# Blocks of 128 tokens of four images with strided weight loads, one copy of x1 by channels, and a 7x7 convolution by image halves

## The chip, the cores and the metric

The kernel runs on one core of a Trainium2 chip. The metric is device time in microseconds (us) of that core, from the first instruction to the last. A core has five engines that run their own instruction streams and meet at semaphores: TensorE (PE in the profile, with its weight loads shown apart as PEld), VectorE (DVE), ScalarE (ACT), GpSimd (POOL) and SyncE (SP). SP and POOL issue nearly all the DMAs here, each in its own queue, in order.

## The reference

The input is `x`, eight images of 96 x 96 positions (tokens) with 192 channels, fp32. Two layers follow, each a residual around a group norm of 32 groups (6 channels each, statistics over a whole image):

```python
# layer 0
proj  = einsum('bhwd,dc->bhwc', gn(x), W_in) + b_in          # 192 -> 384 channels
local = depthwise 3x3 convolution of proj
mixed = 0.25 * (lr + rl + tb + bt) + local                   # four exponential scans of local
x     = x + layernorm(mixed) @ W_out + b_out                 # 384 -> 192; called x1 below
# layer 1
y     = depthwise 7x7 convolution of gn(x1) + dw_bias
y     = layernorm(y) @ w0 + b0                               # 192 -> 768
out   = x1 + (gelu(y) @ w1 + b1) * gamma                     # 768 -> 192
```

## The kernel before

Five passes run one after the other. Pass A normalises `x` and projects it, pass B does the 3x3 convolution and the scans and leaves the mixed 384 channels in the DRAM tile `M_d[w, channel, image, h]`. The change leaves both alone, apart from the size of a zero pad. The passes that it touches are the third (C), the fourth (D) and the fifth (E). All of them run in a written order (`tc.manual_schedule()`): each engine executes its instructions in the order in which the program issues them, and the DMA queues of SP and POOL do the same.

**Pass C (L784 to L1006)** applies layer norm and the output projection and forms x1. A unit is two columns w (3 apart) of a pair of images: four blocks of 96 tokens, one for each column and image, 192 units in all. `load_c` fetches the mixed values (`mt`, 128 channels on the partitions, three such slices) and the tokens of `x` (`xr`), three units ahead. In `block_c`, `mt` is PE's stationary operand (loaded as weights, 96 contiguous columns): three transposes (L850) bring the 384 channels of a block into a PSUM tile `pt`, and three fp32 matmuls (L852, two instructions each) multiply the same weights with `wc`, 192 output channels and one column for the mean. ACT takes the mean (L856) and the sum of squares (L859). One unit later `scale_c` forms the inverse deviation (a power on POOL, L867) and `finish_c` scales the result, adds `xr` and writes `x1u` (L875).

x1 is then stored twice. `X2_d` holds it token by token, for pass E, and goes out from POOL (L884). A DVE copy (L888) turns it into `x1c`, channels outside, and `store_c` (L945) sends it to `X1_d` in 16 pieces for each third of an image pair; this is the form that the convolution reads. DVE's `bn_stats` (L904) on `x1c` give the second group norm's statistics, which `group_steps` turns into scale and shift in `s1`.

**Pass D (L1015 to L1118)** is the 7x7 convolution. Columns are split by w modulo 3 (`PH = 3`), so that a band matrix (`band`, at most 63 x 64) convolves rows and column phases at once, with three matmuls for the remaining column shifts. The 96 rows are cut into six overlapping bands of 21 rows; two bands lie on partitions 0 to 63 and 64 to 127. An iteration handles 12 channels of all eight images: `load_d` (L756) fetches 6 channels, half by SP and half by POOL, `scale_d` (L1028) applies the group norm in place, `conv_d` (L1039) issues 36 matmuls for a channel pair with 256 or 248 moving columns (L1052) and evicts with ACT (L1063), `store_d` (L1071) writes `Y_d`. There are 16 iterations and five buffers for the loads. The first load is issued at the end of pass C.

**Pass E (L1132 to L1317)** is the channel MLP. A unit is 768 tokens: 96 positions h on the partitions, for four columns of an image pair, 96 units. `load_y` fetches a tile of `Y_d`, `stats_e` and `norm_e` do the layer norm on DVE (L1182, L1192), `turn_in` transposes on PE (L1207), `first_layer` runs the 192 to 768 matmuls with 384 moving columns (L1224, L1234) and the gelu on ACT (L1243), `second_layer` runs the matmuls back (L1254, stationary `g`, 192 moving columns), adds the residual `r` on DVE (L1261) and stores from POOL (L1272). `load_r` fetches the residual from `X2_d`; `bias_r` adds the output bias to it on POOL (L1171). Two units are prepared ahead of PE.

## Time and profile before

| | us |
|---|---|
| median of 3 runs (lowest, highest) | 5808.24 (5808.04, 5816.35) |
| span of the profiled execution | 5807.5 |
| PE, PEld busy | 5564.8, 3970.0 |
| DVE, ACT, POOL busy | 3481.9, 2427.7, 2555.8 |
| passes A and B, to the first transpose of C | 1833.9 |
| pass C, first to last matmul | 1018.7 |
| from there to the first convolution matmul | 39.7 |
| pass D, first to last matmul | 444.7 |
| from there to the first matmul of the MLP | 44.1 |
| pass E, to the end | 2426.4 |

The profiled execution's own time is its span, as the first and last instructions bound both. Its page counts an engine as busy while an instruction runs; the end of a matmul is modelled, and matmuls overlap, so a PE near 100% says only that PE had no gap. A row of a group gives line, engine, operation, tiles (output from inputs), shape and count, then busy time and the mean of one in ns, then the idle time ahead of it and what ended that. The DMA share is how busy the 16 DMA engines were. HBM read 574.97 MB and was written 476.72 MB.

### The profile page before, as it was taken

What the parts mean: (1) busy time and instruction counts of PE and PEld (TensorE: products, weight loads), DVE (VectorE), ACT (ScalarE), POOL (GpSimd) and SP (SyncE); (2) the same over time, 40 slices, a digit from 0 to 9 for tenths busy, and PEclk for the clock granted to TensorE, in tenths of its full rate; (3) what the DMA queues carried; (4) which work ended last, traced back from release to release, by engine and by line L of the source; (5) the groups of instructions that cost most, each with busy time, mean ns of one, the idle gap of its engine ahead of it and who ended that gap; (6) DMA issues with size and microseconds to landing.
All of it is one profiled execution on the core that took longest, in us unless ns stands there. A gap on an engine that the chain in (4) does not pass through costs nothing.

```text
span 5807.5 us, 123072 instructions
## 1 busy us (share of the span) xinstructions
PE 5564.8 (96%) x48550; PEld 3970.0 (68%) x48550; DVE 3481.9 (60%) x8079; ACT 2427.7 (42%) x6146; POOL 2555.8 (44%) x2715
## 2 busy tenths in 40 slices
PE   6999989999998999999789869999999999999999
PEld 3666633333335999999678747777777777777777
DVE  5556459999996777777644344444444444444443
ACT  2444447767775666666444412222222222222222
POOL 1111138888886777777523233333233333333232
PEclk9999989999999999999899989999999999999999
DMA  7999779999997999999899842323232222323221
GB/s 209 282 292 267 223 210 245 245 242 242 245 243 207 265 277 283 278 283 277 251 306 333 281 106 65 82 64 81 62 81 66 69 72 64 82 65 82 60 65 40
DMA packets 631724, 1044.28 MB, mean 180 GB/s; under 512 B 108171, under 2 KB 508772, under 8 KB 631148
## 3 DMA queue, kind: packets, MB, share of 16 engines
q1 hardware_dynamic: 515644, 615.70, 40.4%
q0 software_dynamic: 109376, 418.09, 22.3%
q8 instruction: 385, 6.31, 0.5%
q10 hardware_dynamic: 6128, 2.61, 0.2%
q14 instruction: 191, 1.56, 0.1%
HBM read 574.97 MB, written 476.72 MB: 181 GB/s over the span
## 4 chain that ended last, share of the span: by engine, by line
PE 78%; DMA 4%; DVE 2%; issue 1%; POOL 1%; SPq 0%; ACT 0%; POOLq 0%; ACTq 0%; DVEq 0%
PE po L1254 19%; PE po L852 13%; PE hp L1224 13%; PE pl L598 10%; PE hp L1234 7%; PE pa L619 5%; PE pt L850 4%; PE py L1052 3%; PE pa L622 2%; PE pt L1207 2%; DMA xin<-X_d 2%; DMA Y_d<-yo 2%; DVE xin L1037 1%; DMA band<-Z_d 0%; DMA P_d<-po 0%
## 5 line engine op out<-in xcount | busy, mean ns | idle before, releaser
L1243 ACT ACTIVATE g<-hp,b0g 128x384 f32<-128x384 f32 x1152 | 563.3, 587 | 1831.6 <-PE hp L1234 1831.6
L1254 PE MATMUL po<-w1g,g 128*128 128x192 f32 x6912 | 1160.0, 327 | 0.0
L1254 PEld LDWEIGHTS po<-w1g,g 128*128 128x128 f32 x6912 | 1118.8, 190 | 1.1 <-issue 1.1
L852 PE MATMUL po<-wc,mt 128*96 128x193 f32 x4608 | 882.7, 327 | 0.0
L1211 DVE COPY yT<-pt 128x384 f32<-128x384 f32 x288 | 248.6, 863 | 1043.2 <-PE pt L1207 1042.9
L1224 PE MATMUL hp<-yT,w0w 128*128 128x384 f32 x2304 | 781.0, 489 | 0.4 <-DVE yT L1211 0.4
L1272 POOL DMA_DIRECT2D out_dram<-xo x576 | 342.4, 597 | 875.9 <-DVE xo L1261 860.6
L852 PEld LDWEIGHTS po<-wc,mt 128*96 128x96 f32 x4608 | 712.6, 164 | 3.1
L598 PE MATMUL pl<-pin,band 34*32 34x380 f32 (+1 forms) x13824 | 629.7, 489 | 19.9 <-DMA pin<-P_d 18.8
L1224 PEld LDWEIGHTS hp<-yT,w0w 128*128 128x128 f32 x2304 | 429.2, 191 | 257.1 <-issue 2.8
L628 DVE TENSOR_TENSOR_SCAN z<-decay,loc 128x768 f32<-128x768 f32 x288 | 505.8, 1756 | 61.7 <-ACT loc L607 32.1
L668 POOL TENSOR_TENSOR mo<-mo,z 128x768 f32<-128x768 f32 x288 | 529.1, 1837 | 3.4 <-ACT mo L623 0.4
L29 POOL TENSOR_TENSOR rs<-rs_ve,neg_half 96x8 f32<-96x8 f32 x96 | 159.1, 1657 | 823.8 <-DVE rs_ve L28 804.0
L598 PEld LDWEIGHTS pl<-pin,band 34*32 34x32 f32 x13824 | 232.2, 107 | 399.5 <-issue 398.6
L637 DVE TENSOR_TENSOR_SCAN z<-decay,z 128x768 f32<-128x768 f32 x288 | 498.1, 1730 | 0.0
L859 ACT ACTIVATE sq<-pt,mean 96x384 f32<-96x384 f32 x768 | 443.0, 577 | 25.6 <-ACT mean L856 0.8
L1052 PE MATMUL py<-xin,band 63*64 63x248 f32 (+1 forms) x6912 | 389.9, 383 | 62.3 <-DVE xin L1037 44.0
L619 PE MATMUL pa<-loc,mix 128*32 128x384 f32 x3456 | 431.9, 493 | 0.0
L622 PE MATMUL pa<-last,down 96*32 96x384 f32 x1152 | 426.9, 493 | 0.9 <-ACT mo L623 0.9
L1234 PE MATMUL hp<-yT,w0w 64*128 64x384 f32 x2304 | 423.5, 500 | 0.0
L1052 PEld LDWEIGHTS py<-xin,band 63*64 63x64 f32 x6912 | 347.1, 137 | 104.7 <-DVE xin L1037 49.7
L381 PE MATMUL pm<-xT,win 128*128 128x384 f32 x1152 | 394.1, 492 | 9.6 <-DVE po L405 9.6
(118 smaller groups left out, 7659.0 us busy)
## 6 DMA issues: line engine op xcount, KB each, us to landing
P_d<-po POOLq DMA_DIRECT2D x96, 1152.0 KB, 10.2
pin<-P_d SPq DMA_DIRECT2D x192, 576.0 KB
mt<-M_d SPq DMA_DIRECT2D x576, 192.0 KB
xq<-in_x_dram SPq DMA_DIRECT2D x96, 576.0 KB
xr<-in_x_dram SPq DMA_DIRECT2D x384, 144.0 KB
X_d<-x1u POOLq DMA_DIRECT2D x192, 288.0 KB, 4.4
X_d<-x1c SPq DMA_DIRECT2D x192, 288.0 KB
y<-Y_d SPq DMA_DIRECT2D x24, 2304.0 KB
```

The costliest lines, as they stand in the source:

```text
L598: nc.tensor.matmul(pls[g][at * RB : (at + 1) * RB, :, lo:hi], band[rows, c, kh, :], pin[rows, c, :, NJ - 1 - j, lo + kh - 1 : hi + kh - 1] ...
L619: nc.tensor.matmul(pa[at], mix[:, i, at], loc[:, q], start=True, stop=True)
L622: nc.tensor.matmul(pa[at], down[:, to], last[:, q], start=True, stop=True)
L628: nc.vector.tensor_tensor_scan(zf, decay_f, loc.rearrange("p q n -> p (q n)"), 0.0, ALU.mult, ALU.add)
L637: nc.vector.tensor_tensor_scan(zr, decay_f, zr, 0.0, ALU.mult, ALU.add)
L668: nc.gpsimd.tensor_tensor(m, m, z, ALU.add)
L852: nc.tensor.matmul(po[:S, b], lhs[m], wc[:, m], start=(m == 0), stop=(m == NC - 1))
L1052: nc.tensor.matmul(pys[t // 2][g][k * 64 : (k + 1) * 64, t % 2, :, lo:hi], pair[k][0][rows, c, d * ZS : d * ZS + 64], pair[k][1][rows, t, ...
L1224: nc.tensor.matmul(hps[m, q], w0w[:, 2 * q, m * 128 : (m + 1) * 128], yT[:, 2 * q], start=True, stop=False,)
L1234: nc.tensor.matmul(hps[m, q], w0w[p, 1, m * 128 : (m + 1) * 128], yT[p, 1], start=False, stop=True,)
L1243: nc.scalar.activation(g[:, m, q], hps[m, q], AF.Gelu, bias=b0g[:, m : m + 1], scale=1.0)
L1254: nc.tensor.matmul(po[:, q], g[:, m, q, k * 128 : (k + 1) * 128], w1g[:, m], start=(m == 0), stop=(m == NE - 1),)
```

## The change

Pass C works in blocks of 128 tokens taken from four images. The 384 positions (image, h) of one column w of four images are split by index modulo 3, so that a block's weights are every third column of `mt` (`mt[:, m, j::NJ3]`), and its 128 partitions hold 32 positions of each of the four images. A unit is one column of four images, three blocks; 192 units in all. x1 is stored once, in the new `X1_d`, by channels; `X2_d` and the DVE copy are gone, and `finish_c` writes `x1c` directly. Group sums are taken over 32-partition blocks with matmuls against `blk` and `pick`. Pass D runs over image halves (`hf`): 32 iterations of 12 channels of four images, with two buffers of loaded data (`raw`), two of scaled data (`xin`), and 12 matmuls a channel pair of 384 or 372 columns. Its first two loads are issued inside pass C. Pass E uses units of 1,024 tokens (72 units) and reads the residual from `X1_d`.

```diff
-    BP = B // 2
     PH = 3
     WV = S // PH
-    HC = GS
-    X1_d = dram.tile([S * PH + 1, D // HC, BP, HC, WV, 2], F32, name="X1_d")
-    X2_d = dram.tile([BP, PH, S, WV, 2, D], F32, name="X2_d")
+    NH = B // 2
     NV = 2
     WQ = WV // NV
-    Y_d = dram.tile([S * PH, D // HC, BP, NV, HC, 2 * WQ], F32, name="Y_d")
+    GC = 2 * GS
+    NGC = D // GC
+    ROWS = S * PH
+    X1_d = dram.tile([B * ROWS + 1, NGC, NV, GC * WQ], F32, name="X1_d")
+    Y_d = dram.tile([ROWS, 2, GROUPS, NH, NV, GS * WQ], F32, name="Y_d")
...
     s1_pool = ExitStack()
...
+    early = s1_pool.enter_context(tc.tile_pool(name="d_early", bufs=2))
+    s1 = s1_pool.enter_context(tc.tile_pool(name="s1", bufs=1)).tile(
+        [128, 2, NH, 2, GROUPS], F32, name="s1"
+    )
+    def load_d(hf, i):
+        raw = early.tile([128, NT, NH, NV, GC, WQ], F32, tag="raw", name="raw")
+        band = early.tile([128, GC, ZW], F32, tag="band", name="band1")
+        row = NGC * NV * GC * WQ
+        run = NV * GC * WQ
+        for g, eng in enumerate((nc.sync, nc.gpsimd)):
+            for t in range(NT):
                 src = bass.AP(
                     tensor=X1_d.tensor,
...
+                    offset=X1_d.offset
+                    + (hf * NH * ROWS + (2 * t + g) * HG * PH) * row
+                    + i * run,
+                    ap=[[row, 64], [ROWS * row, NH], [1, run]],
                 )
                 eng.dma_start(
...
+                    raw[g * 64 : (g + 1) * 64, t].rearrange("q b a c v -> q b (a c v)"), src
+                )
+        g = i % 2
         (nc.sync, nc.gpsimd)[g].dma_start(
             band[g * 64 : (g + 1) * 64].rearrange("q c l -> q (c l)"),
...
+            Z2_d[:, i * GC : (i + 1) * GC].rearrange("r c l -> r (c l)"),
         )
...
+        return raw, band
...
         def load_c(u):
...
+            hf, p, v = place_c(u)
+            w = v * PH + p
+            mt = ip.tile([128, NC, NH * S], F32, tag="mt", name="mt")
+            nc.sync.dma_start(
+                mt,
+                M_f[S - 1 - w, :, hf * NH * S : (hf + 1) * NH * S].rearrange(
+                    "(m c) n -> c m n", c=128
+                ),
+            )
+            xr = ip.tile([128, NJ3, D], F32, tag="xr", name="xr", bufs=5)
+            nc.sync.dma_start(
+                xr,
+                x_f[hf * NH * S : (hf + 1) * NH * S, w].rearrange("(i j) c -> i j c", j=NJ3),
+            )
+            return mt, xr
+        def block_c(mt, po, var, j):
+            pt = ps_t.tile([128, C], F32, tag="pt", name="pt")
+            lhs = [mt[:, m, j::NJ3] for m in range(NC)]
             for m in range(NC):
...
+                nc.tensor.transpose(pt[:, m * 128 : (m + 1) * 128], lhs[m], ident)
             for m in range(NC):
...
+                nc.tensor.matmul(po, lhs[m], wc[:, m], start=(m == 0), stop=(m == NC - 1))
+            mean = sp.tile([128, 1], F32, tag="mean", name="mean", bufs=4)
+            nc.scalar.copy(mean, po[:, D:])
+            sq = sp.tile([128, C], F32, tag="sq", name="sq", bufs=1)
             nc.scalar.activation(
...
+                sq, pt, AF.Square, bias=mean, scale=-1.0, accum_out=var[:, j : j + 1]
             )
...
+        def finish_c(x1c, v, pos, rs, xr):
+            for j in range(NJ3):
+                nc.vector.scalar_tensor_tensor(
+                    x1c[:, j, :, v],
+                    pos[j][:, :D],
+                    rs[:, j : j + 1],
+                    xr[:, j],
+                    ALU.mult,
+                    ALU.add,
+                )
...
+        NX = 4
+        def store_c(x1c, n, j, q):
+            hf, n = divmod(n, n_s)
+            p, a = divmod(n, NV)
+            r = hf * NH * ROWS + j * PH + p
+            k = slice(q * NGC // NX, (q + 1) * NGC // NX)
             nc.sync.dma_start(
...
+                X1_d[r : r + 127 * NJ3 * PH + 1 : NJ3 * PH, k, a],
+                x1c[:, j].rearrange("i (g c) v -> i g (c v)", c=GC)[:, k],
+            )
+        n_u = 2 * PH * WV
         ahead = [load_c(0), load_c(1), load_c(2)]
         held = x1c = None
...
+        steps, stores, first_d = [], [], []
         with tc.manual_schedule():
             load_weights()
             for u in range(n_u + 1):
...
                     ahead.append(load_c(u + 3))
                 if stores:
                     stores.pop(0)()
+                if u in (n_u - 24, n_u - 12):
+                    first_d.append(load_d(0, len(first_d)))
...
+                    pa = ps_o.tile([128, 2, D + 1], F32, tag="po", name="po")
+                    pb = ps_o.tile([128, 2, D + 1], F32, tag="po", name="po")
+                    pos = [pa[:, 0], pa[:, 1], pb[:, 0]]
+                    for j in range(NJ3):
+                        block_c(mt, pos[j], var, j)
...
+                    n, v = divmod(u - 1, WQ)
+                    if v == 0:
+                        x1c = xp.tile([128, NJ3, D, WQ], F32, tag="x1c", name="x1c")
+                    finish_c(x1c, v, held[0], rs, held[2])
+                    if v == WQ - 1:
+                        steps += group_steps(x1c, n)
+                        stores += [
+                            lambda x=x1c, n=n, j=j, q=q: store_c(x, n, j, q)
+                            for j in range(NJ3)
+                            for q in range(NX)
+                        ]
                 held = (pos, var, xr) if u < n_u else None
...
+        def scale_d(hf, i, raw, band):
+            g = i % 2
             nc.vector.tensor_copy(
                 band[(1 - g) * 64 : (2 - g) * 64], band[g * 64 : (g + 1) * 64]
             )
...
+            xin = xp.tile([128, NT, NH, GC, WV], F32, tag="xin", name="xin")
+            for k in range(2):
+                c = slice(k * GS, (k + 1) * GS)
+                for b in range(NH):
+                    n = 2 * i + k
+                    sc, sh = (s1[:, hf, b, e, n : n + 1] for e in range(2))
+                    for a in range(NV):
+                        nc.vector.tensor_scalar(
+                            xin[:, :, b, c, a * WQ : (a + 1) * WQ],
+                            raw[:, :, b, a, c],
+                            sc,
+                            sh,
+                            ALU.mult,
+                            ALU.add,
+                        )
+            return xin
+        def conv_d(xin, band, c, yo, i):
             pys = [
...
+                ps_y.tile([128, NT * NH, WV], F32, tag="py", name="py") for _ in range(2)
             ]
...
+            for n, d in enumerate((1, 0, 2)):
+                lo, hi = max(0, 1 - d), WV - max(0, d - 1)
+                for k in range(2):
+                    for g in range(2):
+                        rows = slice(g * 64, g * 64 + KB)
+                        nc.tensor.matmul(
+                            pys[g][k * 64 : (k + 1) * 64, :, lo:hi],
+                            band[rows, k * GS + c, d * ZS : d * ZS + 64],
+                            xin[rows, :, :, k * GS + c, lo + d - 1 : hi + d - 1].rearrange(
+                                "q t b v -> q (t b) v"
+                            ),
+                            start=(n == 0),
+                            stop=(n == 2),
+                        )
...
+        def store_d(yo, hf, i, k):
             eng = (nc.sync, nc.gpsimd)[k]
...
+            yf = yo.rearrange("q l n c v -> q l (n c v)")
+            y_d = Y_d[:, hf, 2 * i + k].rearrange("r b a n -> r (b a n)")
+            e = 3 * PH
+            m = HG * PH
+            eng.dma_start(
+                y_d[e : e + NB * m].rearrange("(l q) n -> q l n", q=m),
+                yf[k * 64 + e : k * 64 + e + m],
+            )
+            eng.dma_start(y_d[:e], yf[k * 64 : k * 64 + e, 0])
+            eng.dma_start(y_d[ROWS - e :], yf[k * 64 + KB - e : k * 64 + KB, NB - 1])
+        todo = [(hf, i) for hf in range(2) for i in range(NI)]
         with tc.manual_schedule():
...
+            loads = first_d
+            make_weights(ps_y.tile([128, 512], F32, tag="py", name="ps_b0"))
+            xins = [scale_d(*todo[0], *loads[0])]
             done = None
...
+            for n, (hf, i) in enumerate(todo):
                 if done is not None:
...
+                    store_d(done, *todo[n - 1], 0)
+                if n + 2 < len(todo):
+                    loads.append(None)
+                raw, band = loads[n]
+                xin = xins[n]
                 if done is not None:
...
+                    store_d(done, *todo[n - 1], 1)
+                if n + 1 < len(todo):
+                    xins.append(scale_d(*todo[n + 1], *loads[n + 1]))
+                done = op.tile([128, NB, NH * NV, GS, WQ], F32, tag="yo", name=f"yo_{n}")
+                for c in range(GS):
+                    conv_d(xin, band, c, done, i)
+                if n + 2 < len(todo):
+                    loads[n + 2] = load_d(*todo[n + 2])
             for k in range(2):
...
+                store_d(done, *todo[-1], k)
     s1_pool.close()
...
         def load_y(n):
...
+            hf, p, a, j = place(n)
+            ys[n] = ip.tile([128, D, WQ], F32, tag="y", name=f"y_{n}")
+            r = (NJ3 - 1 - j) * PH + PH - 1 - p
+            q = S // NJ3
+            for b in range(NH):
+                nc.sync.dma_start(
+                    ys[n][b * q : (b + 1) * q].rearrange("h (g c) v -> h g (c v)", c=GS),
+                    Y_d[r :: NJ3 * PH, hf, :, b, a],
+                )
+        def load_r(n):
+            hf, p, a, j = place(n)
+            rs_[n] = ip.tile([128, D, WQ], F32, tag="r", name=f"r_{n}")
+            r = hf * NH * ROWS + j * PH + p
             nc.sync.dma_start(
...
+                rs_[n].rearrange("i (g c) v -> i g (c v)", c=GC),
+                X1_d[r : r + 127 * NJ3 * PH + 1 : NJ3 * PH, :, a],
+            )
+        def bias_r(n):
             nc.gpsimd.tensor_tensor(
...
+                rs_[n], rs_[n], b1g.unsqueeze(2).to_broadcast([128, D, WQ]), ALU.add
             )
...
         def second_layer(u, k):
...
+            n, t = divmod(u, per)
+            hf, p, a, j = place(n)
+            v = t * WE + 2 * k
             nc.vector.tensor_tensor(
...
+                xo[:, k],
+                po,
+                rs_[n][:, :, v : v + 2].rearrange("i c v -> i v c"),
                 ALU.add,
             )
...
             load_y(0)
             load_r(0)
+            load_y(1)
...
+            bias_r(0)
+            load_y(2)
             for u in range(n_u + 1):
+                n, t = divmod(u, per)
                 if u < n_u:
                     first_layer(u, 0)
                 if u + 1 < n_u:
                     turn_in(u + 1, 0)
...
+                if t == 1 and n + 1 < n_y:
+                    load_r(n + 1)
+                    bias_r(n + 1)
                 if u + 2 < n_u:
...
+                    for j in range(WE // 2):
                         stats_e(u + 2, j)
                 if u >= 1:
                     second_layer(u - 1, 0)
+                    second_layer(u - 1, 1)
                 if u + 1 < n_u:
                     turn_in(u + 1, 1)
                 if u < n_u:
...
                 if u + 1 < n_u:
                     turn_in(u + 1, 2)
                 if u + 2 < n_u:
...
+                    for j in range(WE // 2, WE):
                         stats_e(u + 2, j)
                 if u >= 1:
...
+                    second_layer(u - 1, 2)
                 if u + 2 < n_u:
                     for j in range(WE):
                         norm_e(u + 2, j)
+                    if (u + 2) % per == per - 1 and (u + 2) // per + 2 < n_y:
+                        load_y((u + 2) // per + 2)
                 if u >= 1:
...
+                    second_layer(u - 1, 3)
```

## The prediction, made before the changed kernel ran

> **What bounds the kernel now.** I read the 40 slices first, then the stages as stretches of the span, then the groups of instructions by shape, then the DMA issues and the waits. In the slices TensorE (PE) is near 9 everywhere, but DMA is too until slice 23:
>
> ```profile
> PE   6999989999998999999789869999999999999999
> DMA  7999779999997999999899842323232222323221
> ```
>
> I cut the span where the last and first matmuls of the three changed passes lie: third pass (C), gap, convolution (D), gap, last pass (E). Columns: stretch, length, busy us of PE, its weight loads (PEld), DVE, ACT, POOL, granted clock, DMA share, GB/s.
>
> ```profile
> 1833.90:2852.60 1018.70, 1013.30 (x6936) 977.52 (x6936) 752.61 (x2656) 631.41 (x2301) 722.51 (x577) 1.00 0.93 274
> 2852.60:2892.30 39.70, 8.62 (x35) 7.96 (x34) 27.50 (x101) 0.82 (x3) 8.14 (x14) 0.54 0.75 223
> 2892.30:3337.00 444.70, 389.83 (x6912) 347.08 (x6912) 173.30 (x279) 199.93 (x383) 123.53 (x223) 0.94 0.93 307
> 3337.00:3381.10 44.10, 3.42 (x13) 1.96 (x13) 9.30 (x27) 0.82 (x2) 17.53 (x33) 0.54 0.98 221
> 3381.10:5807.50 2426.40, 2414.18 (x12661) 1845.80 (x12660) 1113.25 (x2949) 564.62 (x1153) 748.58 (x767) 1.00 0.26 68
> ...
> 1900.00:2800.00 900.00, 895.34 (x6146) 864.59 (x6145) 677.42 (x2406) 559.79 (x2040) 641.57 (x513) 1.00 0.94 278
> 2950.00:3300.00 350.00, 315.34 (x5629) 276.81 (x5625) 145.54 (x234) 163.41 (x314) 108.99 (x195) 0.96 0.99 335
> ```
>
> C is bound by PE with DMA close behind (0.94), D by DMA (0.99 while PE idles 10%), E by PE alone. The stretches and 1833.9 us ahead of them (passes A and B, untouched) add to the span, 5807.5 us; the median of the runs, 5808.24, is 0.7 above it, so I treat them as one.
>
> ```profile
> L852 PE MATMUL po<-wc,mt 128*96 128x193 f32 x4608 | 882.7, 327 | 0.0
> L852 PEld LDWEIGHTS po<-wc,mt 128*96 128x96 f32 x4608 | 712.6, 164 | 3.1
> L850 PE MATMUL pt<-ident,mt 128*96 128x128 f32 x2304 | 377.2, 272 | 18.4 <-DMA mt<-M_d 18.4
> L850 PEld LDWEIGHTS pt<-ident,mt 128*96 128x96 f32 x2304 | 275.9, 125 | 50.3 <-issue 18.2 <-DMA mt<-M_d 1.3
> L1207 PEld LDWEIGHTS pt<-ident,yn 96*128 96x128 f32 x1152 | 114.9, 142 | 155.9 <-issue 145.5 <-DVE yn L1192 5.0 <-DVE yT L1211 3.5
> L1254 PEld LDWEIGHTS po<-w1g,g 128*128 128x128 f32 x6912 | 1118.8, 190 | 1.1 <-issue 1.1
> L598 PEld LDWEIGHTS pl<-pin,band 34*32 34x32 f32 x13824 | 232.2, 107 | 399.5 <-issue 398.6 <-DMA band<-ZB_d 0.6
> ...
> mt<-M_d SPq DMA_DIRECT2D x576, 192.0 KB
> xr<-in_x_dram SPq DMA_DIRECT2D x384, 144.0 KB
> X_d<-x1u POOLq DMA_DIRECT2D x192, 288.0 KB, 4.4
> X_d<-x1c SPq DMA_DIRECT2D x192, 288.0 KB
> ...
> DVE band L1030 <- DMA band<-Z_d: 95.7, 24, 13.2
> ```
>
> The means overlap, so I take spacings from the timeline. A block of C (3 transposes, 6 matmuls) starts every 1.315 us: 6 x 164.6 ns for 193 moving columns, 3 x 109 ns for 128. A matmul lasts as long whether it yields 96 rows or 128. In E, 128-column weight loads last 190 ns but follow each other every 164 (24 matmuls in 3.93 us), so neighbours overlap.
>
> **What the Trainium skill says.** "TensorE: Matmul & The Clock Gate", LDWEIGHTS (loading the stationary operand): time goes by columns, one per 1/1.2 ns. The rows agree: 107 ns for 32 columns, 190 for 128 make 0.865 ns a column, so 128 columns stream in 111 ns; transposes go at (142 - 125)/32 = 0.53, or 68 ns. "SBUF — State Buffer", Specifications (TRN2): full bandwidth wants at least two hits on each 16-byte line. No strided weight load is in this trace. "DMA: Bandwidth & Descriptors", Specifications: full rate wants 512 B or more; no row here isolates this.
>
> **The change, part by part.**
> *C, PE.* 73,728 tokens in blocks of 128 instead of 96: 576 blocks for 768. At 1.315 us that is 757 us for 1010. The weights are now every third element (12 bytes). Lower bound of that cost: nothing. By the two-hits rule 128 columns touch 96 lines, 192 element times for 128, a factor of 1.5 (estimate from that page): 166 ns against the 164.6 of the matmul, 102 against the 109 of a transpose, still covered. At a factor 2, 222 and 136 ns show: 6 x 222 + 3 x 136 = 1.74 us a block, 1002 us. I take "covered", and keep 2 for the range.
> *C, DMA.* Now 1,440 KB a unit of 768 tokens go by (192 units, 283 MB in all); the second copy of x1 goes away (X2_d, and the DVE copy L888, 213 us, which lay beside PE: nothing). What remains, 226.5 MB, is 221,000 packets of 1,024 B on average (M 1,536; x and the x1 store 768), the same mean as now. At 278/0.94 = 296 GB/s this is 765 us, plus 6.0 MB that two load_d now fetch before C ends, 20 us. DMA, at 785, passes PE at 757; with 9 us of start, and a few lost, **C = 800**. The SP queue issues fewer, larger loads, so its waits are no worse. Behind PE, the chain square, variance, power on POOL, finish_c now has to free PSUM within a unit of 3.95 us instead of 5.26. In the timeline the first x1u starts 2.9 us after its unit's last matmul; two of finish_c's strided writes at 0.40 to 0.48 bring it to 3.7 to 3.95, against 3.95 + 0.33 of transposes. Covered by 0.3 us; a miss of 0.2 would cost 192 x 0.2 = 38.
> *Gap C to D.* The last 32 bn_stats, the group sums, make_weights and scale_d stay: **40**, as before. What is late next is only DVE, since both first loads are there.
> *D.* PE: 4608 matmuls of 376 columns on average for 6912 of 251; at 389.8/6912 = 56.4 ns, times 1.5, 390 us: no gain. DVE: 16 scalings of half the size for 8, at some 0.40 us, and the band copy twice as long: 8 us an iteration. DMA: x1 reads 75.5 MB in 1,536 B runs (were 6,144), Y stores 56.6 MB in 3,072 (were 6,144), bands fetched once per half, 20.4 MB for 10.2; 146.6 MB after the prefetched 6.0. With 296 GB/s at 1.0 KB and 335/0.99 = 338 at 5.8 KB a packet costs 8.4 ns + 45.9 per KB on one of 16 engines, hence 456 us. The first two iterations run at PE's 12.2 us, the others at DMA's 15.2. The new wait: band n+1 may start only when convolution n-1 has ended, and on both SP and POOL the stores of n-1 and the raw loads of n+2 are queued behind it; with 8 us of DVE after it the period is at least (12.5 + landing + 8)/2, 15.3 at a landing of 10 (band loads now take 12.5). I take 15.5: 2 x 12.2 + 30 x 15.5 = **490** for 444.7.
> *Gap D to E.* Now 30.6 us pass before DVE's first statistics, because every image pair needs the last stores. After, the first tile is from half 0, stored long before: eviction, 1.5 MB (4,096 packets of 384 B, 7 us, 14 if short ones cost double) beside the last stores, 16 us; then the same 13.5: **30** for 44.1.
> *E.* A unit has 1,024 tokens for 768, 72 units for 96. From the timeline, before: 24 hp at 332 = 7.96, 12 pairs at 357 = 4.28, 72 po at 163.4 = 11.76, 12 transposes at 92 = 1.10; 25.1 us. After, with 107 ns for 128 more columns (a whole transpose of 128 takes 109): 24 x (332 + 107) = 10.5, 12 x (357 + 107) = 5.6, 96 x 163.4 = 15.7, 12 x 109 = 1.3; 33.1 us. 72 x 33.1 + 17.5 of start and end = **2397** for 2426. bias_r on POOL takes one piece of 7 us behind load_r; the power for the next unit and the stores of xo wait behind it, but that power is due near 29 us into the unit. The 384 B loads have two units, 66 us.
>
> Sum: 1834 + 800 + 40 + 490 + 30 + 2397 = **5591**, 217 below now.
>
> **The rivals.**
> (a) *DMA takes more back.* If C gets only its present 278 GB/s and the band loop in D lands at 15 us: C 226.5 + 6.0 MB = 836, period 17.8, D 25 + 534 = 559; 5696. For it: 0.93 in both stages already. Against: full share was held for 350 us in D.
> (b) *Weights show at factor 2*: C 1011; 5802, no change. For it: one 12-byte step opens a new line three times in four.
> (c) *Weights cost more than a factor 2.01*: that is where 870 ns x factor (6 x 111 + 3 x 68) reaches the 1.75 us a block that eats all 217. At factor 3 a block takes 2.61, C 1512, and the kernel **6303**. Against: 164.6 leaves room for 1.5; DVE statistics on a 128-byte step cost 461 ns for 192 where unstrided ones (241 for 96, 290 for 144) point to 339, a factor well under 2.
> (d) *It does less than it says*: the PSUM chain or the prefetch misses, +40 to +60; inside (a)'s numbers.
>
> **How the numbers follow.** Main case 0.64 (own range 5510 to 5660), (a) 0.16, (b) 0.06, (c) 0.10, 0.04 for another way to be slower. The range is 5500 to 5805: the low end is C at PE's 766 and D at 456, both gaps ten shorter; the high end takes in (a) and (b). Faster by over 0.2% (12 us, about what a measurement of this kernel can tell from no change) 0.82; within it 0.04; slower 0.14.
>
> **What would show it.** Right: C's blocks near 1.39 us with DMA share at 0.97 or more, weight loads of 3*128 under 250 ns; D's share near 0.98; E's period 33.1. Wrong: C's PE busy at 100% with PEld the same and DMA below 0.9 (then the weights bind); PE waiting for DVE x1c each unit; D's period above 17.

## The result, and the profile after

The changed kernel takes **5741.22 us** (median of 4 runs, 5738.68 to 5746.34) against 5808.89 for the kernel before (4 runs): a ratio of 0.9884, 95% interval 0.987 to 0.9898. It is faster, as forecast, but by 68 us (1.2%) and not by 217. The profiled execution has a span of 5736.8 us. Its 40 slices, PE and DMA:

```profile
PE   6999989999998999997777779999999999999999
DMA  7999779999997888888899842233232233232221
```

The stages of the kernel after, cut at the same matmuls as before (stretch, length, busy us of PE, PEld, DVE, ACT, POOL, granted clock, DMA share, GB/s): A and B, C, gap, D, gap, E.

```profile
0.00:1820.80 1820.80, 1732.69 (x21998) 790.04 (x21998) 1408.82 (x2076) 1030.18 (x2305) 935.17 (x1103) 0.99 0.89 244
1820.80:2702.00 881.20, 868.47 (x5196) 846.76 (x5196) 405.80 (x1125) 477.31 (x1725) 442.41 (x391) 0.99 0.86 259
2702.00:2743.30 41.30, 9.52 (x39) 8.79 (x38) 23.56 (x59) 0.83 (x3) 6.29 (x2) 0.55 0.40 115
2743.30:3299.40 556.10, 427.96 (x4608) 185.10 (x4608) 240.50 (x535) 200.76 (x382) 122.99 (x198) 0.87 0.94 262
3299.40:3334.80 35.40, 3.96 (x14) 2.32 (x13) 8.98 (x27) 1.05 (x2) 3.36 (x4) 0.56 0.89 184
3334.80:5736.80 2402.00, 2387.07 (x11222) 1683.17 (x11220) 917.05 (x2277) 516.14 (x865) 518.79 (x395) 1.00 0.30 69
```

| stage | before | predicted | after | after minus predicted |
|---|---|---|---|---|
| A and B | 1833.9 | 1834 | 1820.8 | -13 |
| C | 1018.7 | 800 | 881.2 | +81 |
| gap C to D | 39.7 | 40 | 41.3 | +1 |
| D | 444.7 | 490 | 556.1 | +66 |
| gap D to E | 44.1 | 30 | 35.4 | +5 |
| E, with the end of the span | 2426.4 | 2397 | 2402.0 | +5 |

So two passes hold the miss. In C, PE is busy for 868 of 881 us while DMA falls to 0.86; in D the transfers are at 0.94 but move 262 GB/s where they moved 307 before. The groups of pass C (line, engine, operation, shape, count; busy us and mean ns of one; idle time before) show what grew:

```profile
L863 PE MATMUL po<-wc,mt 128*128 128x193 f32 x3456 | 751.8, 354 | 1.2 <-DVE x1c L880 1.2
L863 PEld LDWEIGHTS po<-wc,mt 128*128 128x128 f32 x3456 | 652.9, 261 | 22.0 <-DVE x1c L880 1.4
L861 PEld LDWEIGHTS pt<-ident,mt 128*128 128x128 f32 x1728 | 275.2, 191 | 25.0 <-issue 24.8
```

A strided load of 128 columns (`po`) lasts 261 ns; the contiguous one in pass E lasts 190. The waits of D (engine, what it waited for; us in total, times, longest) show DVE behind the bands and PE behind DVE:

```profile
DVE band L1046 <- DMA band<-Z_d: 225.8, 23, 20.7
...
POOL band L774 <- PE py L1076: 139.4, 15, 12.8
PE py L1076 <- DVE xin L1056: 129.8, 35, 12.1
```

### The profile page after: what moved, and what is told of

It reads as the page before. It is cut to its first block, busy times and chain, and to the rows that moved or that the text cites. A ratio compares the mean times of both kernels' runs of the same rounds, so it can differ in the third digit from the quotient of the medians.

```text
span 5736.8 us, 106371 instructions
## 1 busy us (share of the span) xinstructions
PE 5429.7 (95%) x43070; PEld 3516.2 (61%) x43070; DVE 3004.7 (52%) x6098; ACT 2226.3 (39%) x5282; POOL 2029.0 (35%) x2093
## 4 chain that ended last, share of the span: by engine, by line
PE 75%; DMA 5%; DVE 3%; issue 2%; SPq 1%; POOL 1%; ACT 0%; POOLq 0%; DVEq 0%
PE po L1257 19%; PE hp L1227 12%; PE po L863 11%; PE pl L598 10%; PE hp L1237 7%; PE pa L619 5%; PE pt L861 3%; PE py L1076 3%; DMA raw<-X_d 2%; PE pa L622 2%; PE pt L1210 2%; DMA band<-Z_d 2%; DVE xin L1056 2%; SPq L770 1%; DMA mt<-M_d 1%
## 5 line engine op out<-in xcount | busy, mean ns | idle before, releaser
L1246 ACT ACTIVATE g<-hp,b0g 128x512 f32<-128x512 f32 x864 | 514.9, 695 | 1850.3 <-PE hp L1237 1850.3
L1227 PE MATMUL hp<-yT,w0w 128*128 128x512 f32 x1728 | 768.0, 594 | 0.0
L863 PE MATMUL po<-wc,mt 128*128 128x193 f32 x3456 | 751.8, 354 | 1.2 <-DVE x1c L880 1.2
L1213 DVE COPY yT<-pt 128x512 f32<-128x512 f32 x216 | 148.9, 689 | 1058.6 <-PE pt L1210 1058.5
L863 PEld LDWEIGHTS po<-wc,mt 128*128 128x128 f32 x3456 | 652.9, 261 | 22.0 <-DVE x1c L880 1.4
L1076 PE MATMUL py<-xin,band 63*64 63x372 f32 (+1 forms) x4608 | 428.1, 516 | 134.6 <-DVE xin L1056 129.8
L1275 POOL DMA_DIRECT2D out_dram<-xo x288 | 210.5, 731 | 894.4 <-DVE xo L1267 877.1
L1267 DVE TENSOR_TENSOR xo<-po,r 128x384 f32<-128x384 f32 x288 | 231.7, 805 | 369.0 <-PE po L1257 369.0
L1076 PEld LDWEIGHTS py<-xin,band 63*64 63x64 f32 x4608 | 185.1, 144 | 377.0 <-issue 281.1
L1237 PE MATMUL hp<-yT,w0w 64*128 64x512 f32 x1728 | 409.8, 606 | 0.0
```

Source lines behind the costliest of these rows:

```text
L863: nc.tensor.matmul(po, lhs[m], wc[:, m], start=(m == 0), stop=(m == NC - 1))
L1076: nc.tensor.matmul(pys[g][k * 64 : (k + 1) * 64, :, lo:hi], band[rows, k * GS + c, d * ZS : d * ZS + 64], xin[rows, :, :, k * GS + c, lo + ...
L1227: nc.tensor.matmul(hps[m, q], w0w[:, 2 * q, m * 128 : (m + 1) * 128], yT[:, 2 * q], start=True, stop=False,)
L1237: nc.tensor.matmul(hps[m, q], w0w[p, 1, m * 128 : (m + 1) * 128], yT[p, 1], start=False, stop=True,)
L1246: nc.scalar.activation(g[:, m, q], hps[m, q], AF.Gelu, bias=b0g[:, m : m + 1], scale=1.0)
```

## The experiments

Where no number of runs is given, a time is that of one run. The parts are compared by stage, since an edit shows there. How far a stage repeats by itself: C takes 881.2, 881.8 and 880.4 us in the kernel after, in d1_band3 and in d2_runs, which hold the same weight loads.

### Pass C: the weight loads

Three kernels differ from the kernel after in one place, the step between the 128 columns of a block's weights: 1, 2 and 4 elements instead of 3 (a block then holds other tokens than the x that is added to it).

```diff
-            lhs = [mt[:, m, j::NJ3] for m in range(NC)]
+            lhs = [mt[:, m, j * 128 : (j + 1) * 128] for m in range(NC)]                             # c1_contig
+            lhs = [mt[:, m, 64 * j + j % 2 : 64 * j + j % 2 + 255 : 2] for m in range(NC)]           # c2_step2
+            mf = mt.rearrange("c m n -> c (m n)")                                                    # c4_step4
+            lhs = [mf[:, 256 * m + j : 256 * m + j + 509 : 4] for m in range(NC)]
```

**c1_contig.** 

> Pass C takes its weights as 128 neighbouring columns (so tokens land in wrong places; instructions, shapes and DMAs stay). Theory W, the 12-byte step makes the weight loads last 262 ns instead of 190 and they bind C: load mean back to about 190 ns, block 1.315 us instead of 1.49, pass C 790 to 810 us instead of 881, now with DMA share above 0.93; the whole 70 to 90 us faster. Rival, blocks of 128 are slow for another reason (the release of PSUM, ACT, the queues): load mean may fall, but C stays above 860.

**c2_step2.** 

> Weights with a step of 2 elements (8 bytes; wrong tokens). If full rate needs two hits on each 16-byte line: as contiguous, load about 190 ns, block 1.315 us, C 790 to 810. If cost grows with the step: load near 225 ns, block about 1.40, C near 840.

**c4_step4.** 

> Weights with a step of 4 elements (16 bytes, one element in each line; wrong tokens). If each new line costs 1.9 ns (183 ns over the 96 lines of step 3): 244 ns of streaming, load mean about 320 ns, block 1.9 us, C about 1110 us, slower than the kernel before. If a factor of 1.65 holds for any step: like the changed kernel, 262 ns and C 881.

Times 5690.58, 5682.38 and 5928.91 us, spans 5688.7, 5680.5 and 5927.0. The instructions that write `po` in each (duration in ns least/median/most, first and last start in us), first c1_contig, then c2_step2, then c4_step4:

```profile
L863 PEld LDWEIGHTS po<-wc,mt x3456: 186/190/338, 1821.4 to 2643.3; 128*128 128x128 f32 x192
```

```profile
L863 PEld LDWEIGHTS po<-wc,mt x3456: 192/197/338, 1817.8 to 2647.0; 128*128 128x128 f32 x192
```

```profile
L864 PEld LDWEIGHTS po<-wc,mt x3456: 307/329/338, 1821.1 to 2888.6; 128*128 128x128 f32 x192
```

C takes 823.0, 830.2 and 1068.5 us for 881.2 at step 3, and its DMA share goes the other way, 0.92, 0.91 and 0.70: the weights bind C, not the transfers. C of c1_contig, columns as in the stages above:

```profile
1820.90:2643.90 823.00, 802.34 (x5196) 756.98 (x5196) 405.90 (x1125) 477.38 (x1726) 441.48 (x391) 0.98 0.92 277
```

How fast the loads follow each other is read from the starts of PE's groups (start us, us, engine, instruction), first in the kernel after, then in c4_step4:

```profile
2061.95 0.49 PE L861 MATMUL pt<-ident,mt 128*128 128x128 f32 x3
2062.36 1.37 PE L863 MATMUL po<-wc,mt 128*128 128x193 f32 x6
2063.56 0.50 PE L861 MATMUL pt<-ident,mt 128*128 128x128 f32 x3
2063.90 1.27 PE L863 MATMUL po<-wc,mt 128*128 128x193 f32 x6
2065.00 0.49 PE L861 MATMUL pt<-ident,mt 128*128 128x128 f32 x3
```

```profile
2064.34 1.61 PE L864 MATMUL po<-wc,mt 128*128 128x193 f32 x6
2065.78 0.51 PE L862 MATMUL pt<-ident,mt 128*128 128x128 f32 x3
```

Six `po` loads and their matmuls take 1.10 us at step 3 (2063.90 to 2065.00), 183 ns each, and 1.44 us at step 4, 240 ns each. At step 1 they follow at 164.6 ns, the pace of the moving columns. By the rule that the prediction cites, what counts is the 16-byte lines that the columns touch: 96 at step 3 and 128 at step 4, 1.9 ns a line in both. Up to step 4 the bytes that the columns span grow exactly as the lines do, so these runs do not tell whether it is lines or span that costs; a step above 4 was not tried. Step 2, 64 lines, stays near the matmul's own time: its blocks start every 1.33 us for 1.315. Contiguous loads save C 58 us, and 23 of its miss remain. All three forecasts of C were missed. c1 and c2 lie above the 790 to 810 of their first theory, by less than the wait that the next section finds; c4 lies 42 below its 1110, as its three transposes take 0.35 us and so hardly more than contiguous ones, 0.33. (c2 is shorter than c1 in all by 8 us, through passes D and A, which the edit does not touch.)

### Pass C: the order of three blocks in two PSUM tiles

With contiguous loads a block should take 1.315 us and a unit 3.95, but a unit takes 4.13. The weight loads of one unit of c1_contig in the timeline (start us, us, engine, instruction, and in brackets the idle time before it and its releaser):

```profile
2063.60 0.41 PEld L861 LDWEIGHTS pt<-ident,mt 128*128 128x128 f32 x3
2064.17 0.96 PEld L863 LDWEIGHTS po<-wc,mt 128*128 128x128 f32 x6 [0.16 <-ACT mean L865]
2065.10 0.41 PEld L861 LDWEIGHTS pt<-ident,mt 128*128 128x128 f32 x3
2065.48 0.96 PEld L863 LDWEIGHTS po<-wc,mt 128*128 128x128 f32 x6
2066.42 0.41 PEld L861 LDWEIGHTS pt<-ident,mt 128*128 128x128 f32 x3
2066.80 0.96 PEld L863 LDWEIGHTS po<-wc,mt 128*128 128x128 f32 x6
```

One `po` group in three starts 0.16 us late, just as ACT has copied `mean` out of the block before. The code says why: a unit's blocks lie at `pos = [pa[:, 0], pa[:, 1], pb[:, 0]]`. Block 1 writes into the tile that ACT still reads for block 0, in the other half of it; if the wait is kept for whole tiles, that is the reason. Before, four blocks alternated between two tiles. The kernel after does not list this wait, yet there too (the lines from 2061.95 us on, above) the `po` group of a unit's second block starts 0.41 us after its transposes, those of the others 0.34, and lasts 1.37 us for 1.27. p1_pos changes the order alone, in the kernel after:

```diff
-                    pos = [pa[:, 0], pa[:, 1], pb[:, 0]]
+                    pos = [pa[:, 0], pb[:, 0], pa[:, 1]]
```

**p1_pos.** 

> The kernel after, with the three PSUM places of a unit's blocks taken in the order pa, pb, pa instead of pa, pa, pb, so that no block follows another in the same tile. Shared-tile theory: the second block no longer waits for ACT's mean of the first, a unit takes 3 x 1.435 = 4.31 us instead of 4.48, and C is 845 to 852 us instead of 881; all else within 5 us, so a span near 5705. Rival (the late start comes from the unit's other waits, or the transfers take it back): C stays at 870 or more.

5720.93 us, span 5719.1. Pass C and pass D of p1_pos, columns as in the stages above:

```profile
1818.10:2670.70 852.60, 833.51 (x5196) 832.07 (x5196) 406.40 (x1126) 477.83 (x1726) 441.94 (x391) 0.99 0.90 267
...
2711.70:3282.30 570.60, 424.76 (x4608) 183.69 (x4608) 240.64 (x535) 200.78 (x382) 122.47 (x198) 0.86 0.92 255
```

C falls by 28.6 us, and every block now starts 1.435 us after the one before. So the order of the places was the cause. Pass D, which this edit does not touch, came out at 570.6. It is the same in the kernel after, c1, c2, c4 and p1 and took 556, 567, 554, 561 and 571 us there, so D's length varies by 17 us between kernels in which it is the same; why is not shown. The total moved less than expected.

### Pass D: bands or reads

```diff
# d1_band3: three band buffers, so that band n+1 needn't wait for convolution n-1
-        band = early.tile([128, GC, ZW], F32, tag="band", name="band1")
+        band = early.tile([128, GC, ZW], F32, tag="band", name="band1", bufs=3)
# d2_runs: the four images of a half side by side in X1_d, reads of 6,144 B for 1,536
-    X1_d = dram.tile([B * ROWS + 1, NGC, NV, GC * WQ], F32, name="X1_d")
+    X1_d = dram.tile([2 * ROWS + 1, NGC, NH, NV, GC * WQ], F32, name="X1_d")
...
-                    ap=[[row, 64], [ROWS * row, NH], [1, run]],
+                    ap=[[row, 64], [1, run]],
# d3_share: one band for both halves (d23_both: d2_runs and this)
...
-        todo = [(hf, i) for hf in range(2) for i in range(NI)]
+        todo = [(hf, i) for i in range(NI) for hf in range(2)]
# d4_writes: d2_runs, and six rows of a partition together in Y_d
...
-                y_d[e : e + NB * m].rearrange("(l q) n -> q l n", q=m),
+                y_d[e : e + NB * m].rearrange("(q l) n -> q l n", q=m),
```

d3_share also issues D's second load behind C's last stores instead of inside C.

**d1_band3.** 

> Three band buffers in pass D instead of two, so that a band can be asked for one convolution earlier. Theory R, D's DMA engines are full (share 0.98) and slow because x1 comes in 1,536 B runs: pass D stays within 10 us of 556. Rival B, the wait for the band after the convolution sets the period (DVE waited 226 us for bands): D falls to 500 or less, with GB/s above 300.

**d2_runs.** 

> X1_d holds the four images of a half side by side in a row, so that load_d reads runs of 6,144 B instead of 1,536; the store in C and load_r in E go in pieces of 32 partitions, 768 B runs as before. Theory R, run length sets D's DMA rate: 310 to 335 GB/s instead of 270, pass D 460 to 500 us. Rival B (band loop) or a limit of 64-partition transfers: D stays at 540 to 560.

**d3_share.** 

> Pass D takes both halves of a channel group one after the other, and a band is loaded and copied once for both: 10.2 MB fewer, and no band is waited for behind a convolution. Theory R: 142 MB at 270 GB/s, pass D 515 to 525 us. Rival B: D below 500.

**d23_both.** 

> Long runs and shared bands together. Theory R: 142 MB at 330 GB/s, 430 us of transfers, so pass D 430 to 460 us, PE (428 us busy) nearly level. Rival B: no better than shared bands alone.

**d4_writes.** 

> The kernel d2_runs with the rows of pass D's output stored in another order, so that each partition's six rows lie together in DRAM (18,432 B in a run instead of six of 3,072 B); the output tokens are then in the wrong order, bytes and instructions are the same. In d2_runs D took 501.6 us at 290 GB/s, in the kernel before 444.8 us at 307 GB/s with writes of 6,144 B. If the length of the writes is what is left, D falls to 470 to 485 us; if only the length of the reads counts, D stays at 495 to 508.

Times 5765.45, 5686.41, 5728.08, 5668.55 and 5693.06 us. The stretch of pass D in d1_band3, in d2_runs, in d3_share, in d23_both and in d4_writes:

```profile
2753.30:3324.00 570.70, 410.82 (x4608) 178.44 (x4608) 241.22 (x535) 199.99 (x382) 134.88 (x198) 0.84 0.94 255
```

```profile
2743.80:3245.40 501.60, 425.31 (x4608) 183.66 (x4608) 241.10 (x535) 200.83 (x382) 109.77 (x198) 0.92 0.96 290
```

```profile
2735.00:3285.20 550.20, 411.23 (x4608) 179.80 (x4608) 218.04 (x519) 200.09 (x382) 121.13 (x191) 0.84 0.92 247
```

```profile
2745.10:3228.60 483.50, 413.96 (x4608) 179.96 (x4608) 217.85 (x519) 200.14 (x382) 109.33 (x191) 0.91 0.95 281
```

```profile
2746.50:3260.20 513.70, 426.25 (x4608) 184.51 (x4608) 240.07 (x535) 201.08 (x382) 108.97 (x198) 0.89 0.91 283
```

The loop through the band buffer, with which the forecast set D's period, is not what holds D: a third buffer takes nothing off. Longer reads take off 54 us at the same bytes, three times D's own variation. What the DMA engines moved in D, in the kernel before, the kernel after and d2_runs:

```profile
DMA packets 29939, 136.35 MB, mean 307 GB/s; under 512 B 7476, under 2 KB 7476, under 8 KB 29871
DMA packets 53905, 145.53 MB, mean 262 GB/s; under 512 B 6584, under 2 KB 31064, under 8 KB 51935
DMA packets 33745, 145.53 MB, mean 290 GB/s; under 512 B 6584, under 2 KB 6584, under 8 KB 31775
```

By their shares in D, 0.93, 0.94 and 0.96, the 16 engines were busy for 414, 523 and 482 us; a packet took one of them 221, 155 and 228 ns on average. The forecast's formula gives 217, 132 and 206 ns for packets of these mean sizes (4.55, 2.70 and 4.31 KB). It is right for the D that it was fitted to and some 22 ns a packet too low for both new ones. With long reads there are 20,160 packets fewer; at the formula's 8.4 ns and these 22 that is 38 us of 16 engines, and 41 were saved. d2's edit changes the length of the reads, the number of packets and the distance of the images in DRAM together, and no run separates these.

Fewer bytes alone gain 6 us, inside D's variation; on top of long reads they gain 18, and D takes 476.8 to 483.5 us in the four kernels with both (d23_both and the three of the last section). Longer writes gain no time: d4's D is 12 us longer than d2's, inside the variation, though its engines were busy for less, 0.91 x 513.7 = 467 us. The forecasts under theory R were right in direction and too hopeful in size: d2 was to take 500 at most, d3_share 525 and d23_both 460; d4 met neither of its ranges. Why a packet costs 22 ns more here than in the kernel before, and so what separates 290 GB/s from 307, is not settled; d4 gives no sign that it is the writes of 3,072 B.

### Passes A and B: 13 us that no edit there explains

In the kernel before, DVE's fill of `mean_w`, from pass C's preparation, stands at 93 us among the instructions of pass A. Waits of the kernel before between 60 and 110 us:

```profile
DVE mean_w L808 <- DMA X_d<-pad: 14.3, 1, 14.3
...
PE pm L381 <- DVE po L405: 9.6, 1, 9.6
```

DVE waits there for the pad's store, whose memory the tile takes over, and PE waits for DVE. In the kernel after, that fill stands at 773 us and PE has no such gap. Two edits of the kernel before, and d1_band3 by accident, touch this.

```diff
# b4_pad
-        pad = zp.tile([S, D * WV * B // S], F32, name="pad")
+        pad = const.tile([S, D * WV * B // S], F32, name="pad")
# b5_mean: filled at the start, in the constant pool (the fill in pass C's preparation is gone)
...
+    mean_w = const.tile([128, 128], F32, name="mean_w")
+    nc.vector.memset(mean_w, 1.0 / C)
```

**b4_pad.** 

> The kernel before, with the zero pad kept in a buffer of its own. There, preparation of pass C was placed into pass A's freed buffers, and DVE and SP waited 14 us for the pad's store (79 to 93 us). If that wait is why passes A and B took 13 us longer before: 8 to 13 us faster, around 5797. If not (the preparation still waits for other stores of the same time): no change.

**b5_mean.** 

> The kernel before with mean_w in the constant pool, filled at the start, instead of in pass C's preparation, where its fill stood at 93 us on VectorE behind a 14.3 us wait. If that wait is what pass A lost, A+B to the first transpose of C is 1820 to 1826 us instead of 1834 to 1835, and the wait is gone from the list; everything after it is unchanged, so 10 to 14 us less in all. Rival (the 13 us come from elsewhere, another order of pass C's instructions or transfers): A+B stays at 1832 or more, or another instruction of pass C's preparation stands there and waits in its place.

Times 5803.37 and 5803.95 us beside 5806.27 and 5804.9 for before. Both fell short, and their waits in the same stretch tell why, b4_pad first, then b5_mean:

```profile
DVE mean_w L808 <- DMA Z_d<-z: 13.7, 1, 13.7
```

```profile
DVE lnb L813 <- DMA gb<-in_L_conv_ln_b_dram: 9.2, 1, 9.2
```

Take away the pad, and the fill waits for the next store from the same pool; take away the fill, and the next instruction of that preparation waits. A and B took 1835.1 and 1830.9 us. In d1_band3 the fill is back at 93 us, waits 13.2 us, and A and B take 1830.3; in the other eleven kernels built on the one after, the fill stands at 770 to 774 us, and A and B take 1817 to 1824. Where pass C's preparation falls thus goes with about 10 of the 13 us. What moved it was not isolated; other sizes in memory are a guess.

### A version that beats both

v1_blocks and v2_blocks make the contiguous loads of c1_contig yield the right tokens, on top of d23_both: pass B writes `M_d` in the order in which C's blocks want it. v1 makes a block of 32 neighbouring rows of four images, v2 keeps every third row. v3_order adds p1's order of PSUM places.

```diff
# v2_blocks, pass B (v1_blocks: "(b j h)" for "(b h j)", and x loaded in three DMAs a unit)
...
-                nc.scalar.copy(mo[:, i, q], pa)
+                nc.scalar.copy(
+                    mo[:, i, q].rearrange("p (j b h) -> p j b h", j=NJ, b=GB),
+                    pa.rearrange("p (b h j) -> p j b h", b=GB, j=NJ),
+                )
...
```

**v1_blocks.** 

> The kernel after with x1 in 6,144 B runs and the bands shared by both halves (d23_both), and with blocks whose 128 tokens lie next to each other: pass B writes M so that a block is 32 rows of four images in a row (its add on GpSimd is cut in two for that, twice the instructions of half the size), the x loads of a unit are three instead of one, and the output leaves in two DMAs of one image column instead of one of two. Weights theory: pass C's po loads at 190 ns, C at 800 to 825 us instead of 872, D unchanged at 475 to 490, E within 5 us of 2403, so a span of 5605 to 5630, against 5666.8 of d23_both. Rival: pass C is held by its transfers, not by the weights, or the additional DMA issues and adds cost as much: span over 5650.

**v2_blocks.** 

> The kernel d23_both, with M written by pass B in the order (token within three, image, row), so that the 128 tokens of a block lie next to each other and everything else of pass C and E is as in d23_both; B's copies on ScalarE and its adds on GpSimd (cut in two, twice the instructions) read at a step of three elements. In v1_blocks it was the x loads, three a unit with a step in two levels, that held pass C (SP's queue never waited long, GpSimd waited 528 us of 1000 for x); here they are one a unit again. Weights theory: po loads 190 ns, C at 800 to 825 us against 872.7, D and E unchanged, span 5605 to 5630. Rival: the steps of three slow pass B, A+B over 1835, and eat half of the gain or more.

**v3_order.** 

> The kernel v2_blocks (contiguous weights, long reads, bands shared) with the same order of PSUM places. There DMA has a share of 0.91 in C at 278 GB/s. Shared-tile theory with PE still the bound: C 770 to 785 us instead of 808.4, span 5570 to 5590. Rival (transfers bind from here on): C at 790 to 808, span 5590 to 5607, with PE waiting for mt.

v1_blocks: 5959.89 us (5 runs), a ratio of 1.0262 to before (1.0239 to 1.0284). Its loads last 190 ns and still C takes 1173.8 us:

```profile
1820.80:2994.60 1173.80, 854.68 (x5196) 766.23 (x5196) 405.76 (x1125) 477.46 (x1725) 439.44 (x387) 0.97 0.72 192
```

The x loads in v1_blocks, and in the kernel after:

```profile
L860 SPq DMA_DIRECT2D xr<-in_x_dram x576: 528/1149/6160, 1816.9 to 2986.2; - x192
...
  POOL xr L1012: 630.0, 191
```

```profile
L850 SPq DMA_DIRECT2D xr<-in_x_dram x192: 545/551/2584, 1817.2 to 2684.6; - x192
```

Three issues of 1,149 ns a unit, each for a third of the bytes with the rows in two levels, keep SP's queue busy for more than half of the 6.1 us that a unit now takes; `mt` and the x1 stores are issued between them, and POOL waits 630 us for x. SP's queue itself waited for others in 121 us of the 1,000 from 1900 to 2900, in the kernel after in 525 of the 800 from 1900 to 2700, so it had become what C waits for. Why one such issue takes twice as long was not isolated; the shortest took 528 ns. v2_blocks loads x once a unit again and takes 5609.04 us, a ratio of 0.9662 (0.9649 to 0.9676). v3_order takes **5574.78 us**, a ratio of 0.9607 (0.959 to 0.9624), 2.9% below the kernel after. Its stages (gaps left out; that from C to D takes 53.0 us, 12 more than in the kernel after, as in d23_both):

```profile
0.00:1822.80 1822.80, 1733.28 (x21998) 790.15 (x21999) 1410.98 (x2076) 1030.75 (x2305) 1036.64 (x1391) 0.99 0.89 244
1822.80:2600.30 777.50, 765.41 (x5196) 750.57 (x5196) 405.93 (x1125) 477.56 (x1726) 438.96 (x387) 0.99 0.93 289
...
2653.30:3133.40 480.10, 414.50 (x4608) 181.02 (x4608) 217.25 (x519) 200.39 (x383) 108.28 (x191) 0.92 0.95 283
...
3167.00:5571.80 2404.80, 2388.99 (x11221) 1684.26 (x11220) 917.05 (x2277) 516.15 (x865) 518.63 (x395) 1.00 0.34 69
```

C is at 576 x 1.315 = 757 us plus 20, as PE waits 22.7 us for `mt` in three places, and DMA at 289 GB/s still follows. POOL's adds in pass B, cut in two and read at a step, cost it 101 us of busy time more (1036.6 for 935.2), and A and B at most some 4 us.

## Why the prediction was right and wrong

**C, the weights: the step that failed first.** The text priced a load of every third column by the rule of "SBUF — State Buffer", Specifications (TRN2), at 166 ns, and called that covered by a matmul's 164.6. Nothing was left over, so every ns above showed. It measured 183, 10% above the estimate: six loads and three transposes make 1.435 us a block for 1.315, and 576 x 0.12 = 69 us. For the `po` loads the small cost of step 2 and the cost at steps 3 and 4 have the form of that rule; only the price of a line was too low, 166/96 = 1.73 ns for 1.9. The loads for transposes do not go by lines: they last 196, 191 and 208 ns at steps 2, 3 and 4. The sign named for it, C's PE at 100% with DMA below 0.9, is what the profile shows. Rival (b) had the mechanism with too large a factor, 2 for 183/111 = 1.65.

**C, a wait that was not seen.** The chain behind PE was judged by whether finish_c frees a tile within a unit, and that held: PE waits 1.2 us for `x1c` in all. But the three blocks of a unit were put into two tiles, two neighbours into one, and 192 units lose 0.17 us each, 33 us; p1_pos took back 29 of them. The prediction itself put 0.2 us a unit at 38 us, for the other end of the chain. So C is 757 + 69 + 33 and 22 of start and waits for `mt`, 881; the text had 757 and 43 more, for transfers that would bind, the start and small losses. Without the two failed steps it would have been close: v3_order, with one of D's loads less inside C, takes 777.5 us for 800.

**D: the price of a packet, the other step that failed.** The formula of 8.4 ns and 45.9 per KB was drawn from mean packets of 1 KB in C and 5.8 in D, and gave 456 us of transfers. The 146 MB were right. But the engines were busy for 523 us, at 155 ns a packet for the formula's 132, and stood idle for 33 us of D's 556, mostly at its two ends (from 2800 to 3250 us their share was 0.98). In C the formula still held in the kernel after: 225,080 packets of 1.01 KB at a share of 0.86 took 54 ns each, the formula gives 55. So it did not carry over to D's new transfers, and d2_runs, with reads four times as long, takes back 54 us of time but not the 22 ns a packet. What makes a packet dearer there was not found. The 490 itself came from the bands' loop, 34 us above the transfers, and d1_band3 opens that loop and gains nothing. That d2_runs' 501.6 lies 12 from the forecast is therefore luck: for its packets the formula gives 435. Rival (a)'s 559 for D was met by number, but not by its own reason, a loop through the band landing at 15 us. PE's 390 us of busy time became 428 at a clock of 0.87; it had not been the bound.

**Right.** The gap C to D (41.3 for 40), the gap D to E (35.4 for 30) and E (2402 for 2397, from spacings of 332 + 107 and 357 + 107 ns). The text's own terms of E, 72 x 33.1 + 17.5, make 2401, so that its sum is 4 too low and E was met even better. The removed DVE copy was called worth nothing; PE waited 1.2 us for DVE in C, but no run put the copy back. **Not foreseen:** the 13 us of pass A.

**The sum.** +81 and +66 are the miss; with -13 of A and B and +12 of the gaps and E they make 146, the distance from 5591 to the span of 5736.8.

## What to carry to other kernels

Before a stationary operand is taken at a step, price its load and leave a margin to the matmul that should cover it: here the 16-byte lines that its columns touch cost 1.9 ns each, and from step 3 on the load was slower than the matmul. The instructions that produce the data may be able to write the wanted order; here they did so for some 4 us. If a PSUM tile holds two blocks, let no two neighbours in time share it: here that cost 0.17 us a unit. And a layout that makes one consumer's transfers simpler should be priced by the number and length of the other's reads. A price per packet that was fitted to two stages held for one of them and was 22 ns too low for the changed other.

## What the runs showed of the hardware

- `po` weight loads of 128 columns: 190 ns contiguous, 197 at a step of two elements, 262 at three, 329 at four. The loads for transposes behave differently: 139 contiguous, 196 at two, 191 at three, 208 at four.
- The same 145.5 MB in pass D move at 262 GB/s with reads of 1,536 B in runs and at 290 with 6,144 B, at DMA shares of 0.94 and 0.96. The share does not tell the two apart; the packets do, 53,905 and 33,745.
- An x load of 96 KB whose rows come in two levels kept SP's queue for 1,149 ns (median in v1_blocks, the least 528); one of 288 KB with plain rows for 551 (the kernel after, the least 545).
